# Turning the first four x tiles on TensorE, in a fused cross-attention and feed-forward kernel

## The chip, the cores and the metric

The kernel runs on one core of one Trainium2 chip. The metric is the device time of one execution in microseconds (us). A few times are given in nanoseconds (ns). Engines are named as in the profile: PE is TensorE's matmul, PEld its weight load, DVE is VectorE, ACT is ScalarE, POOL is GpSimd, SP is SyncE, and SPq is SyncE's queue, which issues all DMAs here.

## The reference

Two batches of x (1024 x 2048, f32) and of a context ctx (2048 x 2048, f32). Each passes through two blocks with a residual:

```python
def fake_quant(x, s, z):
    return (clip(round(x / s + z), 0, 255) - z) * s

x = x + fake_quant(layernorm(x), s1, z1) @ fake_quant(ctx, s2, z2)
xf = layernorm(x)
# router: softmax over 8 experts, the two largest, scaled to sum 1 -> w (zero elsewhere)
h = einsum('td,erd->ter', xf, lora_A)
lora = einsum('ter,eor,te->to', h, lora_B, w) * 2.0
x = x + xf @ W_base.T + b_base + lora
```

The change touches only the first line: the layernorm of x, its quantisation and the way it gets to TensorE in the first product.

## The kernel before

A tile is 128 rows of x, so a batch has eight, i = 0 to 7. The first product (GEMM1) contracts over 2048 rows of ctx, 16 steps of 128, named k. It writes four column blocks of 512, named c0 to c3. One unit (i, c) is 16 matmuls of 128x128 by 128x512 into one PSUM bank. All matmuls take f16; the quantised values are small integers.

**From x to the stationary operand (ln1).** Each tile is loaded in two halves of 1024 columns (h = 0, 1); tile 0 of batch 0 in four pieces. VectorE takes batch statistics (L387) and a first guess of the reciprocal root (L393 to L401). Newton steps refine it (L412 to L423), and three small operations (L616 to L618) make scale and offset. [...] Then ScalarE writes q as uint8, which rounds and clips, and ScalarE or VectorE subtracts the zero point and writes qn as f16. The matmul needs the tile with k on the partitions, so a DMA transpose (L356, on SyncE's queue) writes aT (in the profile `at`). Tile 0 of batch 0 has one for each half, every other tile one for the whole:

```python
            if b == 0 and i == 0:
                transpose(... HD)      # one for each half h
        if b or i:
            transpose(aT.ap, qn.ap, [qn], [aT], D)
```

**From ctx to the moving operand (load_b).** Each column block is loaded in eight parts of 512 KB (`bs`, L352). For each part, one operation writes u as uint8 and one writes b as f16. Both go through `affine` (L366 on ScalarE, L375 and L377 on VectorE), which the planner may put on either engine.

**Warm-up.** When the first half of qn of tile 0 is there, TensorE runs WARM = 30 matmuls on it, whose result is not used.

**GEMM1 and after.** gemm1 issues a unit in groups of two or four k (L670), and VectorE adds the result to x (L691). Batch 0 goes through tiles 0 to 3 for all four columns first, then 4 to 7. After a tile's four units comes its second layernorm (ln2, y_prep): f32 combinations, split into a high and a low f16 part (`nat`) and turned by a DMA transpose (`y`). The second product (GEMM2, L1119) is a Strassen-like scheme over those, with the weight prepared in the same way (w_step, L931), after a short one for the router (hmm, `ph`, L819 and L823). w_norm reads the whole weight once for a scale (`wn`).

**Order.** The kernel's body only adds tasks to a Plan: for each task an engine or a choice of engines, an assumed duration, the buffers it reads and writes, and a priority. Priorities are due times, worked backwards from the due time t of the matmuls. Plan.order then plays the program through greedily. At each moment every free engine takes the ready task with the smallest priority that fits into the buffers. The instructions are issued in the order that comes out, and each engine runs its own in order, so that an instruction which waits holds all those behind it. For a DMA transpose the plan lets SyncE be busy until all earlier DMAs have landed. The warm-up task has priority 0.0. Buffers come from slots: 48 of 4 KB per partition (`u`), and eight PSUM banks (`ps`).

Of the kernel before, what the change touches and what calls it, by code (L numbers as in the profile page):

```python
# [12 lines left out]
F16 = mybir.dt.float16  # L13
# [8 lines left out]
P = 128  # L22
# [7 lines left out]
HK = KT // 2  # L30
# [4 lines left out]
HD = D // 2  # L35
# [9 lines left out]
LANES = 8  # L45
DEPTH = 2.5
NEAR = 45.0
WARM = 30
WFAR = 90.0
HFIRST = (0, 2, 4)  # L50
HLATE = (6, 1, 3, 5, 7)
EV1 = 5.0
SP_D = 10.0
HC = 4.0
PUT = 10.0
# [36 lines left out]
class Plan:  # L92
# [3 lines left out]
    def add(self, eng, dur, fn, r=(), w=(), prio=None, cap=None, dma=None, far=None, turn=False):  # L96
        t = Task()
        t.durs = eng if isinstance(eng, dict) else {eng: dur}
        t.eng, t.dur = None, min(t.durs.values())
        t.fn, t.prio, t.cap, t.dma = fn, prio, cap, dma  # L100
        t.preds, t.succs, t.bufs = set(), [], []
        t.seq, t.ready, t.start, t.done = len(self.tasks), 0.0, None, None
        t.pe = prio if eng == "PE" else None
        t.far, t.turn = far, turn

        def spans(accs):
            for a in accs:
                buf, parts = a if isinstance(a, tuple) else (a, None)
                if buf not in t.bufs:
                    t.bufs.append(buf)  # L110
                    buf.users += 1
                for i in range(buf.parts) if parts is None else parts:
                    yield buf, i

        for buf, i in spans(r):
            last, readers = buf.state[i]
            if last is not None:
                t.preds.add(last)
            readers.append(t)
        for buf, i in spans(w):  # L120
            last, readers = buf.state[i]
            if last is not None:
                t.preds.add(last)
            t.preds.update(readers)
            buf.state[i] = (t, [])
        t.preds.discard(t)
        for p in t.preds:
            p.succs.append(t)
        self.tasks.append(t)
        return t  # L130
# [14 lines left out]
    def order(self):  # L145
        self.rank()
        free = dict(SLOTS)
        busy = dict.fromkeys(("SP", "ACT", "DVE", "POOL", "PE"), 0.0)
        ready = {e: [] for e in busy}
        events = [0.0]  # L150
        lanes = []
        dma_free = 0.0
        land = 0.0
        lag = 0.0
        for t in self.tasks:
# [5 lines left out]
        first = set()  # L161
# [36 lines left out]
        while todo:  # L198
# [8 lines left out]
            for eng in busy:  # L207
                while busy[eng] <= now:
                    pick = None
                    q = ready[eng]  # L210
                    for n, item in enumerate(q):
                        t = item[2]
                        if t.ready > now:
                            continue
                        h = t.far if t.far is not None else HORIZON
# [19 lines left out]
                    t = pick  # L235
# [9 lines left out]
                    if t.dma is not None:  # L245
                        if t.turn:
                            end = max(end, land)
                            dma_free = max(dma_free, end + t.dma)
# [33 lines left out]
def xattn_ffn_kernel(ctx, tc, x, cx, scal, wT, bias, arT, bT, out):  # L282
    nc = tc.nc
# [13 lines left out]
    def bank(name):  # L297
        return Buf(
            "ps", lambda: psum.tile([P, C], F32, tag="mm", bufs=SLOTS["ps"], name=name),
            name=name,  # L300
        )

    def fixed(t, parts=1):
# [26 lines left out]
        out=ident, in_=ident, pattern=[[-1, P]], compare_op=ALU.not_equal, fill=1.0, base=0,  # L330
        channel_multiplier=1,
    )
    iota = const.tile([P, E], F32)
    for e in range(E):
        nc.gpsimd.memset(iota[:, e : e + 1], float(e))
# [19 lines left out]
    def transpose(dst, src, r, w, cols, **kw):  # L355
        add("SP", 1.35 + 0.25 * cols / 1024, lambda: nc.sync.dma_start_transpose(dst(), src()),  # L356
            r=r, w=w, dma=0.5 * cols / 1024, turn=True, **kw)

    def affine(dst, src, n, r, w, scale=None, bias=None, only=None, **kw):
        ptrs = sum(v is not None and not isinstance(v, float) for v in (scale, bias))  # L360

        def fn(eng):
            get = lambda v: v() if callable(v) else v
            o, i, a, c = dst(), src(), get(scale), get(bias)
            if eng == "ACT":
                nc.scalar.activation(  # L366
                    o, i, AF.Copy if c is None else AF.Identity,
                    scale=1.0 if a is None else a, bias=0.0 if c is None else c,
                )
            elif a is None and c is None:  # L370
                nc.vector.tensor_copy(o, i)
            elif c is None:
                nc.vector.tensor_scalar(o, i, a, None, ALU.mult)
            elif a is None:
                nc.vector.tensor_scalar(o, i, c, None, ALU.add)  # L375
            else:
                nc.vector.tensor_scalar(o, i, a, c, ALU.mult, ALU.add)  # L377

        durs = {"ACT": n * 0.00083 + 0.19 + 0.09 * ptrs, "DVE": n * 0.00053 + 0.145 + 0.06 * ptrs}
        if only:  # L380
            return add(only, durs[only], lambda: fn(only), r=r, w=w, **kw)
        return add(durs, 0, fn, r=r, w=w, **kw)
# [217 lines left out]
    def ln1(S, b, i):  # L600
        n = f"{b}_{i}"
        xt = S["x", i]
        s = buf("sm", [P, 52], F32, f"sm1_{n}")
        for h in range(2):
            add("DVE", 1.3, lambda h=h: stats(xt[h], s, 0, h), r=[xt[h]], w=[s])
        add("DVE", 0.8, lambda: rstd_seed(s, 1), w=[s])

        fast = b == 0 and i == 0

        def newton():  # L610
            e = nc.vector if fast else nc.gpsimd
            rstd_newton(e, s, 1)
            a = s.ap()
            r = a[:, 4:5]
            m = a[:, 48:49]
            e.tensor_tensor(a[:, 10:11], r, r1, ALU.mult)  # L616
            e.tensor_tensor(a[:, 11:12], m, a[:, 10:11], ALU.mult)
            e.tensor_tensor(a[:, 12:13], z1, a[:, 11:12], ALU.subtract)  # L618

        add("DVE" if fast else "POOL", 2.2 if fast else 4.0, newton, w=[s])  # L620
        aT = buf("u", [P, KT, P], F16, f"at_{n}", 2)
        qn = buf("u", [P, D], F16, f"qn_{n}", 2)
        for h in range(2):
            q8 = buf("q8", [P, HD], U8, f"q8_{n}_{h}")
            affine(q8.ap, xt[h].ap, HD, [xt[h], s], [q8],
                   scale=lambda: s.ap()[:, 10:11], bias=lambda: s.ap()[:, 12:13],
                   only="ACT")
            affine(lambda h=h: qn.ap()[:, h * HD : (h + 1) * HD], q8.ap, HD, [q8], [(qn, [h])],
                   bias=nz1)
            if b == 0 and i == 0:  # L630
                transpose(
                    lambda h=h: aT.ap()[:, h * HK : (h + 1) * HK, :],
                    lambda h=h: qn.ap()[:, h * HD : (h + 1) * HD],
                    [(qn, [h])], [(aT, [h])], HD)
        if b or i:
            transpose(aT.ap, qn.ap, [qn], [aT], D)
        S["at", i] = aT
        if fast:
            warm = bank("warm")

            def warm_up():
                for _ in range(WARM):
                    nc.tensor.matmul(
                        warm.ap(), qn.ap()[:, :P], qn.ap()[:, :C], start=True, stop=True
                    )

            add("PE", MM * (WARM + 8), warm_up, r=[(qn, [0])], w=[warm], prio=0.0)

    def load_b(S, b, c):
        for j in range(4):  # L650
# [627 lines left out]
```

## Time and profile before

| what | us |
|---|---|
| median of 3 runs (957.34 to 962.02) | 958.4 |
| the profiled execution | 959.11 |
| its span in the profile | 957.3 |
| PE busy | 909.2 |
| DVE busy | 712.4 |
| ACT busy | 418.9 |
| POOL busy | 85.1 |

The mean granted clock of TensorE in the profiled execution is 0.994 of full speed. The queue of DMAs carries 242.33 MB and takes 83.7% of the 16 DMA engines' span; HBM moves 213 GB/s over the span. Before the first matmul of the warm-up there are 17.03 us, and the first of GEMM1 starts at 25.30.

In the profile's rows a time in brackets is how long the engine sat idle before that row, with what released it. A wait for several things is put down to the one that came last. Idle time of an engine that is not the bottleneck costs nothing by itself. Windows of a few microseconds count the DMA share of 16 engines, so a value near 1 is a full stretch.

### The profile page before, as it was taken

Reading aid. Unit: us, or ns where it says so; the run is one execution under the profiler, and the core shown is the slowest. Engines: PE = TensorE matmul, PEld = TensorE weight load, DVE = VectorE, ACT = ScalarE, POOL = GpSimd, SP = SyncE. Lnnn points to the kernel's source line nnn. Section 1 sums busy time; section 2 is a strip of 40 time slices with the busy share of each in tenths; the row PEclk is TensorE's granted clock in tenths of the full one; section 3 lists DMA queues with packets and bytes.
Section 4 is the critical chain, followed back from the end, with each engine's and each line's share of the span. In section 5 each row is a group of like instructions: output and inputs, shape, how many; then the busy total and the mean of one; then the engine's idle time right before and its main releaser. Section 6 shows DMA issues by size and latency. Waiting matters only on the chain.

```text
span 957.3 us, 12424 instructions
## 1 busy us (share of the span) xinstructions
PE 909.2 (95%) x4484; PEld 431.6 (45%) x4484; DVE 712.4 (74%) x1224; ACT 418.9 (44%) x473; POOL 85.1 (9%) x352
## 2 busy tenths in 40 slices
PE   2799998999989999999999999998999999999998
PEld 1244445465434444444444444644644444444443
DVE  7579758998878885999464765899938996599331
ACT  4598658823436242333566664671611331224000
POOL 2305212000000000003320122000000000000000
PEclk9999999999999999999999999999999999999999
DMA  9899999699999999966899858899795779893011
GB/s 315 225 391 353 271 304 262 158 217 296 199 311 332 355 339 352 353 206 227 229 252 374 339 155 235 212 218 223 248 226 194 232 243 343 296 382 126 34 70 63
DMA packets 231534, 243.12 MB, mean 254 GB/s; under 512 B 160816, under 2 KB 162864, under 8 KB 231472
## 3 DMA queue, kind: packets, MB, share of 16 engines
q1 hardware_dynamic: 231472, 242.33, 83.7%
q8 instruction: 35, 0.57, 0.2%
q14 instruction: 27, 0.22, 0.1%
HBM read 172.03 MB, written 31.46 MB: 213 GB/s over the span
## 4 chain that ended last, share of the span: by engine, by line
PE 49%; DVE 21%; DMA 18%; issue 5%; POOL 4%; SPq 1%; ACT 1%; DVEq 0%; ACTq 0%; POOLq 0%
PE X L1119 19%; PE Y L1119 13%; PE g L670 12%; DMA wb<-in_wT_dram 5%; DVE w L931 4%; DVE xr L1147 3%; DMA bs<-in_cx_dram 3%; DMA wt<-in_wT_dram 3%; DMA wn<-in_wT_dram 3%; PE ph L819 2%; DMA wc<-in_wT_dram 2%; DVE wb L999 2%; DVE xr L1038 2%; PE X L1135 1%; PE ph L823 1%
## 5 line engine op out<-in xcount | busy, mean ns | idle before, releaser
L670 PE MATMUL g<-b,at 128*128 128x512 f16 x1024 | 225.3, 381 | 9.9 <-DMA at<-qn 7.4
L1119 PEld LDWEIGHTS <-y_s 128*128 128x128 f16 x1536 | 150.2, 98 | 185.9 <-issue 5.6
L1119 PE MATMUL X<-w,y_s 128*128 128x512 f16 x768 | 206.9, 379 | 4.4 <-DVE w L931 2.9
L1119 PE MATMUL Y<-w,y_s 128*128 128x512 f16 x768 | 206.9, 379 | 0.1
L1119 PE MATMUL X<-w,y_a 128*128 128x512 f16 x768 | 189.9, 379 | 3.2 <-DVE w L931 1.6
L1119 PEld LDWEIGHTS <-y_a 128*128 128x128 f16 x1152 | 112.3, 98 | 138.8 <-issue 7.0
L670 PEld LDWEIGHTS <-at 128*128 128x128 f16 x1024 | 100.2, 98 | 132.2 <-DMA at<-qn 9.4
L366 ACT ACTIVATE w<-wb,gW 128x1024 f16<-128x1024 f32 (+1 forms) x64 | 66.0, 1039 | 156.4 <-DVE wb L992 45.8
L1119 PE MATMUL Y<-w,y_a 128*128 128x512 f16 x384 | 103.8, 381 | 1.6 <-DVE xr L1147 1.6
L931 DVE SCALAR_TENSOR_TENSOR w<-wb,gW,w 128x1024 f16<-128x1024 f32 (+1 forms) x64 | 73.0, 1148 | 9.2 <-ACT w L366 9.1
L1147 DVE SCALAR_TENSOR_TENSOR xr<-X,uW,xr 128x512 f32<-128x512 f32 x64 | 46.5, 745 | 30.2 <-PE X L1135 28.7
L366 ACT ACTIVATE u<-bs,sc,rec 128x1024 uint8<-128x1024 f32 x45 | 55.5, 1238 | 25.8 <-DMA bs<-in_cx_dram 23.2
L691 DVE SCALAR_TENSOR_TENSOR x<-g,s,x 128x512 f32<-128x512 f32 x64 | 47.2, 746 | 12.3 <-PE g L670 12.2
L1147 DVE SCALAR_TENSOR_TENSOR xr<-Y,uW,xr 128x512 f32<-128x512 f32 x42 | 31.1, 744 | 31.8 <-PE Y L1135 31.8
L375 DVE TENSOR_SCALAR b<-u,nz 128x1024 f16<-128x1024 uint8 x40 | 29.9, 752 | 29.2 <-ACT u L366 29.1
L366 ACT ACTIVATE w<-wc,gW 128x1024 f16<-128x1024 f32 x23 | 26.2, 1143 | 54.9 <-DVE wc L955 45.4
L387 DVE BATCH_NORM_STATS2 sm<-x 128x6 f32<-128x512 f32 x64 | 40.7, 682 | 12.1 <-DMA x<-in_x_dram 6.2
L366 ACT ACTIVATE q<-x,sm 128x1024 uint8<-128x1024 f32 x32 | 38.5, 1231 | 24.0 <-POOL sm L618 15.0
L412 POOL TENSOR_SCALAR sm<-sm 128x1 f32<-128x1 f32 (+1 forms) x21 | 4.5, 216 | 482.9 <-DVE sm L399 421.2
L709 ACT ACTIVATE sq<-x,sm 128x1024 uint8<-128x1024 f32 x32 | 36.4, 1138 | 19.7 <-DVE sm L702 10.9
L819 PE MATMUL ph<-ar,y_a 128*128 128x272 f16 x192 | 38.2, 292 | 7.0 <-DMA y_a<-nat_a 4.1
L366 ACT ACTIVATE nat_s<-yt_a 128x1024 f16<-128x1024 f32 x32 | 33.0, 1049 | 19.6 <-DVE yt_a L778 11.2
(168 smaller groups left out, 970.6 us busy)
## 6 DMA issues: line engine op xcount, KB each, us to landing
wt<-in_wT_dram SPq DMA_DIRECT2D x80, 512.0 KB, 6.7
bs<-in_cx_dram SPq DMA_DIRECT2D x64, 512.0 KB, 10.5
wn<-in_wT_dram SPq DMA_DIRECT2D x32, 512.0 KB, 8.7
wb<-in_wT_dram SPq DMA_DIRECT2D x32, 512.0 KB, 6.9
x<-in_x_dram SPq DMA_DIRECT2D x30, 512.0 KB, 8.7
spill<-x SPq DMA_DIRECT2D x28, 512.0 KB, 3.8
xr<-spill SPq DMA_DIRECT2D x28, 512.0 KB, 8.3
wc<-in_wT_dram SPq DMA_DIRECT2D x24, 512.0 KB, 7.9
```

Source lines behind the costliest of these rows:

```text
L366: nc.scalar.activation(o, i, AF.Copy if c is None else AF.Identity, scale=1.0 if a is None else a, bias=0.0 if c is None else c,)
L375: nc.vector.tensor_scalar(o, i, c, None, ALU.add)
L387: nc.vector.bn_stats(st[:, 2 * h + c], b.ap()[:, c * C : (c + 1) * C])
L670: nc.tensor.matmul(ps.ap(), aT.ap()[:, k, :], S["b", c, k // 4].ap()[:, k % 4, :], start=k == 0, stop=k == KT - 1,)
L691: nc.vector.scalar_tensor_tensor(xs, ps.ap(), s12, xs, ALU.mult, ALU.add, accum_out=s.ap()[:, o : o + 1])
L709: nc.scalar.activation(sq.ap(), xb.ap(), AF.Square, bias=a[:, 22 + j : 23 + j], accum_out=a[:, 24 + 2 * j + h : 25 + 2 * j + h],)
L819: nc.tensor.matmul(ph.ap()[:, : 2 * AR], y[half].ap()[:, 0, k, :], ar[:, kr, :], start=kk == 0, stop=False,)
L931: lambda: nc.vector.scalar_tensor_tensor(w.ap()[:, 1, lo:up], src(), g, w.ap()[:, 0, lo:up], ALU.mult, ALU.subtract),
L999: lambda: nc.vector.tensor_tensor(bot.ap(), bot.ap(), top.ap(), ALU.subtract),
L1038: lambda xb=xb: nc.vector.tensor_tensor(xb.ap(), xb.ap(), bb.ap(), ALU.add),
L1119: nc.tensor.matmul(ps.ap(), y.ap()[:, a, k, :], w.ap()[:, q, j * C : (j + 1) * C], start=k == 0 and fresh and i == 0, stop=k == HK - 1 and ...
L1147: nc.vector.scalar_tensor_tensor(xs, ps.ap(), uW[:, cp : cp + 1], xs, ALU.mult, ALU.add)
```

## The change

For tiles 0 to 3 of batch 0 (TURNS = 4) the DMA transposes fall away. In their place comes `turn`, once for each half: eight TensorE transposes of 128x128, with an f16 identity made once by GpSimd, into one PSUM bank read as f16, and one `affine` that copies the bank to aT, on ScalarE or VectorE. For the same four tiles the Newton chain runs on VectorE; before, that held for tile 0 alone. The warm-up has 20 matmuls instead of 30. The planner starts all engines at 0.9 us and its DMA clock at 1.2 us. Tiles 4 to 7 of batch 0, all of batch 1, and the transposes of y stay with the DMA.

```diff
-WARM = 30
+WARM = 20
...
+TURNS = 4
+TMM = 0.12
...
-        busy = dict.fromkeys(("SP", "ACT", "DVE", "POOL", "PE"), 0.0)
+        busy = dict.fromkeys(("SP", "ACT", "DVE", "POOL", "PE"), 0.9)
...
-        events = [0.0]
+        events = [0.0, 0.9]
...
-        dma_free = 0.0
+        dma_free = 1.2
...
+    ident16 = const.tile([P, P], F16)
+    nc.gpsimd.tensor_copy(ident16, ident)
...
-        fast = b == 0 and i == 0
+        first = b == 0 and i == 0
+        pe_turn = fast = b == 0 and i < TURNS
...
-            if b == 0 and i == 0:
-                transpose(
-                    lambda h=h: aT.ap()[:, h * HK : (h + 1) * HK, :],
-                    lambda h=h: qn.ap()[:, h * HD : (h + 1) * HD],
-                    [(qn, [h])], [(aT, [h])], HD)
-        if b or i:
+            if pe_turn:
+                turn(aT, qn, h, n)
+        if not pe_turn:
             transpose(aT.ap, qn.ap, [qn], [aT], D)
         S["at", i] = aT
-        if fast:
+        if first:
             warm = bank("warm")
...
+    def turn(aT, qn, h, n):
+        ps = bank(f"turn_{n}_{h}")
+
+        def mm():
+            for j in range(HK):
+                k = h * HK + j
+                nc.tensor.transpose(
+                    ps.ap().bitcast(F16)[:, j * P : (j + 1) * P],
+                    qn.ap()[:, k * P : (k + 1) * P], ident16,
+                )
+
+        add("PE", HK * TMM, mm, r=[(qn, [h])], w=[ps])
+        affine(
+            lambda: aT.ap()[:, h * HK : (h + 1) * HK, :].rearrange("p k t -> p (k t)"),
+            lambda: ps.ap().bitcast(F16), HD, [ps], [(aT, [h])])
```

## The prediction

> **What bounds the kernel now.** I read the page's busy shares first, then the waits of TensorE, then the timelines of TensorE, of SyncE's queue and of ScalarE over the first 60 us, and last the windows around them. Busy shares:
>
> ```profile
> span 957.3 us, 12424 instructions
> PE 909.2 (95%) x4484; PEld 431.6 (45%) x4484; DVE 712.4 (74%) x1224; ACT 418.9 (44%) x473; POOL 85.1 (9%) x352
> ```
>
> TensorE is idle for 957.3 - 909.2 = 48.1 us in all, so an edit that leaves its matmuls alone can win only from these and from matmuls at a low clock. Its waits (engine and line, what it waited for, total us, times, longest):
>
> ```profile
> PE warm L643 <- ACT qn L366: 17.0, 1, 17.0
> PE g L670 <- DMA at<-qn: 7.4, 4, 3.9
> PE ph L819 <- DMA y_a<-nat_a: 4.1, 2, 3.4
> PE g L670 <- DVE b L375: 1.9, 2, 1.3
> ```
>
> The 17.0 us are the first tile's way to qn, which the change leaves as it is. The next row is the landing of the DMA transposes. TensorE's timeline shows where it lies (start, length, what, and in brackets the idle time before it):
>
> ```profile
> 17.03 8.44 PE L643 MATMUL warm<-qn 128*128 128x512 f16 x30 [17.03 <-ACT qn L366]
> 25.30 1.89 PE L670 MATMUL g<-b,at 128*128 128x512 f16 x8
> 31.11 6.07 PE L670 MATMUL g<-b,at 128*128 128x512 f16 x20 [3.92 <-DMA at<-qn]
> 37.71 2.75 PE L670 MATMUL g<-b,at 128*128 128x512 f16 x12 [0.53 <-DVE b L375]
> 42.89 7.08 PE L670 MATMUL g<-b,at 128*128 128x512 f16 x32 [2.43 <-DMA at<-qn]
> 51.30 29.12 PE L670 MATMUL g<-b,at 128*128 128x512 f16 x134 [1.33 <-DVE b L375]
> ```
>
> By 51.30 only 8+20+12+32 = 72 matmuls are done. In the last row one takes 29.12/134 = 0.217 us, so 72 are worth 15.6 us, yet they took 26.0. The 20 at 31.11 took 6.07 instead of 4.34: the clock had dropped in the gap before. Why the transposes are late stands in SyncE's queue and in ScalarE:
>
> ```profile
> 18.40 3.33 SPq L352 DMA_DIRECT2D bs<-in_cx_dram  x4
> 25.02 15.47 SPq L356 DMA_TRANSPOSE at<-qn  x4
> 40.55 14.68 SPq L352 DMA_DIRECT2D bs<-in_cx_dram  x15
> ...
> 28.05 1.24 ACT L366 ACTIVATE q<-x,sm 128x1024 uint8<-128x1024 f32 x1 [1.90 <-POOL sm L618]
> 34.24 1.24 ACT L366 ACTIVATE q<-x,sm 128x1024 uint8<-128x1024 f32 x1 [2.68 <-POOL sm L618]
> ```
>
> Four transposes stand in the queue one behind another, each waiting for its qn, and from 21.7 to 40.55 no context load goes out behind them. The qn wait for GpSimd's Newton steps: its three chains run from 16.15 to 20.60, to 28.02 and to 34.21, 4.5, 7.5 and 6.2 us. The windows show what it leaves empty (length, busy time of PE, PEld, DVE, ACT, POOL with counts, clock, DMA share, GB/s):
>
> ```profile
> 30.00:40.00 10.00, 8.36 (x31) 3.43 (x32) 6.48 (x12) 6.10 (x6) 3.48 (x10) 0.83 0.47 96
> 60.00:70.00 10.00, 10.00 (x48) 4.52 (x47) 8.73 (x20) 9.83 (x12) 0.00 (x0) 1.00 1.04 392
> ```
>
> The DMA engines are half empty just before a stretch in which they are full (share 1.04) and VectorE and ScalarE nearly so.
>
> **Part by part.** *Removed: five DMA transposes and GpSimd's three Newton chains.* Gone are 3.92 + 2.43 us of waits for at. The waits for b at 37.71 and 51.30 (0.53 + 1.33) come from loads held back behind the transposes: gone with the block, if ScalarE and VectorE convert in time. Gone is the cold clock: 6.07 - 4.34 = 1.7 us. Sum 8.2 + 1.7 = 9.9 us.
>
> *Added on VectorE: three Newton chains.* The first tile's chain, already there, runs from 12.45 to 14.52: 2.07 us, so 6.2 us for three. On GpSimd the same cost 18.2 us, and it was on the path. Queued behind each in VectorE's order are the next tile's statistics (0.64 us each) and the conversions of b.
>
> *Added on TensorE: 64 transposes of 128 columns, in 8 groups of 8.* No row shows one. From below: a 128x136 matmul at L823 is followed by the next after 0.057 us (155.02 to 155.08), 56 x 0.057 = 3.2 us; I count 7 groups, since the first runs ahead of the first matmul. From above: nothing overlaps, and each pays its weight load (0.098 us) and the full length of a 128x136 matmul (0.223 us), 56 x 0.32 = 17.9 us. I take 0.0875 us, half the 0.175 us in which a pair of L819 and L823 with two weight loads repeats, since a transpose needs one load for few columns: 4.9 us. A gain is excluded: it is pure extra work on the engine that sets the end.
>
> One rule speaks against the change. The Trainium skill, "TensorE: Matmul & The Clock Gate", Part 4: PE-mode transpose, gives about 275 ns for a 128x128 transpose inside a kernel and says that transposes don't count as activity for the clock gate. By that the term would be 56 x 0.275 = 15.4 us, an estimate, and the whole change a loss of 3.5 us. This trace shows no transpose; I hold to its rows, because eight in a row to one bank can be pipelined as the pairs at L819 are.
>
> *Added on ScalarE or VectorE: eight evacuations of 128x1024 f16 from PSUM.* Bounds: 0.75 us (L375, as many elements) and 1.23 us (L366 from f32); at 1.0 that is 8 us. With Newton it makes 14.2 us of new work. From 25.3 to 51.3 ScalarE was busy for 13.34 of 26.0 us and VectorE for 12.46, so 26.2 us lie free: it fits, but the c1 conversions (8 parts at 1.23 + 0.75, 16 us) move into the same stretch. 14.2 + 16 exceeds 26.2 by 4 us of two engines, 2 us of time. I charge these 2.0 us as new waits for b or at; bounds 0 and 5.
>
> *Warm-up 20 instead of 30.* The ten dropped matmuls ran at 0.217: 2.2 us, so it ends at 25.47 - 2.2 = 23.3. It has priority 0.0 and stands before the first turn in TensorE's order. Turn 0.7, evacuation 0.75 to 1.15 and some hops: first real matmul at 25.0 to 25.4. Before, it was 25.30. I count nothing: the ten matmuls only hid the transpose's landing.
>
> *Moved: the context loads, up to 19 us earlier.* DMA is full from 40 to 170, and a tile's transpose kept it about 2.4 us (share 0.47 of 10 us for two from 30 to 40). So the work behind runs ahead of need. The small waits later in GEMM1 (0.65 at 81.07, 0.49 at 89.06, 0.15 at 100.63, 0.90 at 104.29; sum 2.2) should mostly go: 1.5 us. At the seam to GEMM2 TensorE waits 4.1 us for y_a; ScalarE, which prepares it, waited 8.2 us for wn loads from 100 to 165. With those earlier I take 2.5 us of the 4.1, bounds 0 and 4.1. What is late next is the chain of the last tile's layernorm, which doesn't depend on loads.
>
> *The planner's clock* starts at 0.9 us for all engines. A uniform shift changes no order by itself. But new durations reorder the greedy plan, and from 164 us on TensorE still idles for 48.1 - 17.0 - 14.5 = 16.6 us, spread over many waits. That can move by about 3 us either way; I count 0. The identity's f16 copy on GpSimd comes at about 2 us, 15 us before use: free.
>
> Sum against the profiled execution's 959.1 us (its span is 957.3): -9.9 + 4.9 + 2.0 - 1.5 - 2.5 = -7.0, so 952.1. The median of the runs is 0.7 lower than that execution, 958.4: 951.4, rounded to **951.5**.
>
> **The rivals.** *The converters take over.* Without the DMA in the way ScalarE and VectorE hold the first two columns, and TensorE waits for b instead of at. For it: 9 tenths busy from 60 to 90. Against: 26 us free before. With 5 us of new waits and nothing won at the seam: -9.9 + 4.9 + 5.0 - 1.5 = -1.5, about 957.
>
> *The transposes don't pipeline.* Place: TensorE's own queue between 23 and 45 us, where seven groups stand between matmuls. At 0.32 us each: -9.9 + 17.9 + 2.0 - 1.5 = +8.5, about 967. It decides from (9.9 - 2.0 + 1.5)/56 = 0.17 us per transpose on. For it: a single 128-column matmul has a length of 0.22 us. Against: the rows at L819 and L823 follow one another at a quarter of that.
>
> *Everything comes back.* Waits for at, the four small ones and the seam go entirely, and transposes cost 0.057: -9.9 - 2.2 - 4.1 + 3.2 = -13, about 945.
>
> *It doesn't do what it says*, if the turns stand in order behind a late qn and hold ready matmuls. TensorE would then wait as long as now; about 958, the same side as the first rival.
>
> **How the numbers follow.** Forecast 0.47 (its own range 948 to 955), everything back 0.18, converters or late qn 0.25, no pipelining 0.10. What a measurement of this kernel can tell from no change is about 0.5%, 4.8 us: faster means below 953.6, slower above 963.2. The forecast gives 0.43 to faster and 0.04 to same; everything back 0.18 to faster; the first rival 0.01 to faster, 0.23 to same and 0.01 to slower; no pipelining 0.10 to slower. Faster 0.62, same 0.27, slower 0.11. The range 944 to 960 leaves out most of the no-pipelining case and the ends of others.
>
> **What would show it.** Right: no wait for at before 55 us, first real matmul near 25, context loads without a gap from 20 to 40, transposes at under 0.12 us from one to the next, 128 matmuls done by about 60 instead of 63.5. Wrong: waits for b of over 5 us in all before 60, or a seam wait larger than 4.1 us, or groups of eight transposes longer than 1.4 us.

## The result, and the profile after

| | before | after |
|---|---|---|
| median of 20 runs each, same chips, us | 959.83 (956.35 to 964.44) | 959.14 (956.49 to 961.82) |
| ratio of after to before, 95% interval | | 0.9989 (0.9977 to 1.0002) |
| span of the profiled execution, us | 957.3 | 957.2 |

No difference that this kernel's measurement can tell, where 951.5 and faster were forecast. The page after, busy shares:

```profile
span 957.2 us, 12516 instructions
PE 912.3 (95%) x4538; PEld 434.5 (45%) x4538; DVE 716.7 (75%) x1255; ACT 423.7 (44%) x480; POOL 71.4 (7%) x305
```

TensorE has 54 matmuls more (64 transposes, 10 warm-up matmuls less), GpSimd is busy 13.7 us less. TensorE's waits (columns as before):

```profile
PE warm L645 <- DVE qn L379: 16.9, 1, 16.9
...
PE Y L1137 <- DVE x L1165: 2.8, 1, 2.8
PE ph L837 <- DMA y_a<-nat_a: 2.7, 2, 1.9
PE X L1137 <- DVE x L1165: 2.5, 1, 2.5
PE g L688 <- DVE b L379: 2.1, 1, 2.1
...
PE turn L657 <- ACT qn L370: 1.2, 1, 1.2
PE g L688 <- ACT at L370: 0.8, 2, 0.6
```

The 7.4 us for `DMA at<-qn` are gone, and what took their place before 60 us is small (2.1 for b, 1.2 for qn, 0.8 for at, now copied by ScalarE). But far behind the change, Y at L1137 waits 2.8 us for VectorE's x at 220 us, which has no counterpart in before, and X waits 2.5 us for it at 769 us, where before waited 1.5:

```profile
PE X L1119 <- DVE x L1147: 1.5, 1, 1.5
```

TensorE's timeline of after at the start:

```profile
23.09 0.61 PE L657 MATMUL turn<-ident,qn 128*128 128x128 f16 x8
24.89 0.62 PE L657 MATMUL turn<-ident,qn 128*128 128x128 f16 x8 [1.20 <-ACT qn L370]
25.80 1.04 PE L688 MATMUL g<-b,at 128*128 128x512 f16 x4 [0.28 <-ACT at L370]
...
29.99 0.59 PE L688 MATMUL g<-b,at 128*128 128x512 f16 x2 [2.06 <-DVE b L379]
...
43.13 40.43 PE L688 MATMUL g<-b,at 128*128 128x512 f16 x186
```

Eight transposes take 0.61 us. One has a length of 0.219 us in the trace, so from one to the next it is (0.61 - 0.219)/7 = 0.056 us. From 43.13 on the matmuls run in one block of 186. SyncE's queue sends the context loads without a hole, 23 from 7.72 to 39.05, and the window from 30 to 40, which had a DMA share of 0.47, is full:

```profile
7.72 31.33 SPq L356 DMA_DIRECT2D bs<-in_cx_dram  x23
```

```profile
30.00:40.00 10.00, 9.44 (x60) 5.12 (x60) 9.48 (x16) 10.00 (x11) 0.00 (x0) 0.83 1.05 387
60.00:70.00 10.00, 10.00 (x48) 4.51 (x46) 10.00 (x21) 9.97 (x12) 3.55 (x11) 1.00 1.04 394
```

**Where the time went.** The order of the instructions behind 156 us is the same on all engines in both kernels, and the matmuls are the same in number, so the n-th can be compared with the n-th. The table gives its start minus that in the first profile of before, us (warm-up, transposes and added dummies not counted; negative is earlier); the columns are the time that this matmul has in before. Kernels below the second row are those of the experiments.

| kernel | 25 | 62 | 113 | 185 | 242 | 353 | 627 | 767 | 953 |
|---|---|---|---|---|---|---|---|---|---|
| after | +0.5 | -2.4 | -5.8 | **-8.1** | -5.2 | -3.7 | -3.7 | -3.0 | **-0.4** |
| after, a second profile (e5) | +0.5 | -2.4 | -5.7 | -7.8 | -3.2 | -3.5 | -3.7 | -3.9 | -1.5 |
| before, a second profile (e9) | 0.0 | -0.3 | -0.2 | -1.9 | -2.1 | +0.4 | +0.2 | +0.7 | +0.1 |
| loads on ScalarE's queue (e1) | +0.1 | -2.8 | -6.1 | -6.9 | -7.2 | -3.3 | -2.7 | -3.4 | -3.3 |
| start 8 us later (e3) | +8.6 | +5.7 | +2.4 | +1.2 | +1.7 | +4.2 | +4.7 | +6.0 | +8.5 |
| Newton alone (e4) | +0.6 | -2.9 | -4.8 | -6.8 | -6.7 | -4.8 | -5.0 | -4.4 | -5.2 |
| turn alone (e10) | -0.1 | +0.9 | -2.4 | -7.4 | -3.6 | -2.1 | -1.9 | -1.2 | +2.2 |
| after, 74 dummies (e13) | +0.4 | -2.5 | -5.8 | -8.7 | -7.5 | -5.6 | -6.1 | -5.5 | -5.5 |
| Newton alone, 54 dummies (e14) | +0.8 | -3.1 | -4.2 | -4.0 | -4.2 | -1.2 | -1.6 | -2.7 | -1.9 |
| before, 54 dummies (e16) | -0.4 | -1.2 | -1.0 | -0.4 | -0.6 | +1.6 | +1.3 | +0.9 | +1.6 |

The gain is there at 185 us, 8.1 us, more than the 7.0 forecast. Then it is given back: 2.8 us by 242, 1.6 by 353, 0.6 by 767 and 2.7 just behind it. The third row says how far to trust one row: two profiles of the same kernel stand up to 2.1 us apart at these columns, though these two agree at the end (the two of after end 1.1 us apart).

**The loss at 220.** SyncE's queue ahead of it, before and after:

```profile
210.18 0.53 SPq L352 DMA_DIRECT2D wt<-in_wT_dram  x1
210.76 3.32 SPq L356 DMA_TRANSPOSE y_s<-nat_s  x1
...
220.96 0.53 SPq L352 DMA_DIRECT2D wt<-in_wT_dram  x1
```

```profile
202.79 0.96 SPq L356 DMA_DIRECT2D wt<-in_wT_dram  x1
203.80 5.24 SPq L360 DMA_TRANSPOSE y_s<-nat_s  x1
...
215.94 0.53 SPq L356 DMA_DIRECT2D wt<-in_wT_dram  x1
```

The first wt load goes out 7.4 us earlier than before, but the transposition behind it holds the queue for 5.24 us instead of 3.32, and the next wt load goes out only 5.0 us earlier. VectorE waits for that one, and TensorE for VectorE:

```profile
220.65 0.69 DVE L964 TENSOR_TENSOR wb<-wt 128x512 f32<-128x512 f32 x1 [1.72 <-DMA wt<-in_wT_dram]
...
222.40 0.74 DVE L1165 SCALAR_TENSOR_TENSOR x<-Y,uW,x 128x512 f32<-128x512 f32 x1
```

```profile
223.19 0.81 PE L1137 MATMUL Y<-w,y_s 128*128 128x512 f16 x3 [2.75 <-DVE x L1165]
```

So the first 2.8 us went into a transfer that was never on TensorE's path in the forecast. Before had the same wait of VectorE, with TensorE far enough behind for it not to matter:

```profile
225.88 0.69 DVE L946 TENSOR_TENSOR wb<-wt 128x512 f32<-128x512 f32 x1 [1.67 <-DMA wt<-in_wT_dram]
```

The size of TensorE's wait is about what its lead (8.1 us) exceeds the lead of that wt load by (5.0). Why the transposition ahead of it takes longer is the question of the last experiments.

### The profile page after: what moved, and what is told of

It reads as the page before. It is cut to its first block, busy times and chain, and to the rows that moved or that the text cites. A ratio compares the mean times of both kernels' runs of the same rounds, so it can differ in the third digit from the quotient of the medians.

```text
span 957.2 us, 12516 instructions
## 1 busy us (share of the span) xinstructions
PE 912.3 (95%) x4538; PEld 434.5 (45%) x4538; DVE 716.7 (75%) x1255; ACT 423.7 (44%) x480; POOL 71.4 (7%) x305
## 4 chain that ended last, share of the span: by engine, by line
PE 62%; DVE 18%; DMA 11%; issue 3%; SPq 3%; ACT 3%; POOL 1%; DVEq 0%; ACTq 0%
PE X L1137 23%; PE g L688 18%; PE Y L1137 16%; DMA wb<-in_wT_dram 5%; DVE w L949 3%; SPq L360 2%; DVE xr L1165 2%; DMA wc<-in_wT_dram 2%; DMA wn<-in_wT_dram 2%; PE X L1153 2%; DVE nat_s L789 2%; DVE xr L1056 1%; PE ph L837 1%; DVE wb L979 1%; DVE sm L391 1%
## 5 line engine op out<-in xcount | busy, mean ns | idle before, releaser
L1137 PEld LDWEIGHTS <-y_s 128*128 128x128 f16 x1536 | 150.5, 98 | 188.8 <-issue 9.9
L1137 PE MATMUL X<-w,y_s 128*128 128x512 f16 x768 | 207.7, 380 | 2.9 <-ACT w L370 1.4
L1137 PE MATMUL Y<-w,y_s 128*128 128x512 f16 x768 | 207.5, 380 | 2.9 <-DVE x L1165 2.8
L1137 PE MATMUL X<-w,y_a 128*128 128x512 f16 x768 | 192.0, 382 | 4.8 <-DVE x L1165 2.5
L1137 PEld LDWEIGHTS <-y_a 128*128 128x128 f16 x1152 | 112.7, 98 | 142.0 <-issue 11.5
L1137 PE MATMUL Y<-w,y_a 128*128 128x512 f16 x384 | 103.8, 381 | 1.6 <-DVE xr L1165 1.6
L370 ACT ACTIVATE u<-bs,sc,rec 128x1024 uint8<-128x1024 f32 x47 | 57.5, 1234 | 17.8 <-DMA bs<-in_cx_dram 13.4
L561 ACT ACTIVATE wn<-wn 128x1024 f32<-128x1024 f32 x22 | 23.2, 1053 | 45.6 <-DMA wn<-in_wT_dram 45.6
```

Of the source, the lines that this page charges most:

```text
L370: nc.scalar.activation(o, i, AF.Copy if c is None else AF.Identity, scale=1.0 if a is None else a, bias=0.0 if c is None else c,)
L561: nc.scalar.activation(d.ap(), s.ap(), AF.Square, accum_out=o)
L1137: nc.tensor.matmul(ps.ap(), y.ap()[:, a, k, :], w.ap()[:, q, j * C : (j + 1) * C], start=k == 0 and fresh and i == 0, stop=k == HK - 1 and ...
```

## The experiments

Times are medians, in brackets the ratio to runs of before on the same chip and its 95% interval. The texts on record name their theories by letters of their own; the verdicts below are in words.

**e1 and e2, the weight loads of the second group on ScalarE's queue.** In the kernel after (e1) and, as a control, in the kernel before (e2), the loads wt and wb of group 1 are issued by ScalarE, so that no transposition stands ahead of them:

```diff
-    def load(dst, dst_ap, src, nbytes, w, r=(), **kw):
-        add("SP", 0.42, lambda: nc.sync.dma_start(dst_ap(), src() if callable(src) else src),
+    def load(dst, dst_ap, src, nbytes, w, r=(), queue=None, **kw):
+        q = queue or nc.sync
+        add("SP", 0.42, lambda: q.dma_start(dst_ap(), src() if callable(src) else src),
...
+    Q1 = nc.scalar
...
-                top = load_wrow(k, cp, f"wt_{n}", far=WFAR)
+                top = load_wrow(k, cp, f"wt_{n}", far=WFAR, queue=Q1)
...
-                     C * 4, [(s, [0])])
+                     C * 4, [(s, [0])], queue=Q1)
```

> The changed kernel, with the weight loads of the second group of the second product (first column half, both batches) issued from ScalarE's queue instead of SyncE's; nothing else, same order. The changed kernel starts its second product 8.1 us earlier than the kernel before, and loses 2.8 us of that at one wait at 220 us, where VectorE waits for a weight load (wt) that stands in SyncE's queue behind two transposes of y. Theory A (the lead is lost at single places, each held by a chain that came forward less than TensorE): the wait of 2.8 us at 220 falls under 0.5, the lead after it stays at 7 to 8 us instead of 5.2, some of it is lost at the next place (320 us, the sum of the weight's squares), and the whole is 1 to 3 us below the changed kernel, about 956 to 958. Theory B (what follows is bound by the total work of the DMA engines and VectorE, so that any lead is lost): the lead is back at 5 us by 260, and the whole stays within 0.5 us of the changed kernel.

> The control for the run with weight loads on ScalarE's queue: the same edit on the kernel before. TensorE has no wait at that place there. Theory A: nothing to win at 220; total within 1 us of the kernel before, 958 to 960. Theory B: the same. A gain of over 2 us would mean that moving the loads is worth something by itself, and that the comparison has to be made against this kernel.

Measured: e1 957.13 (0.9974, 0.9953 to 0.9996), e2 959.42 (0.9982, 0.9962 to 1.0003). In e1 there is no wait at 220, and the lead stands at 242 with 7.2 us; in the kernel before the same edit changes nothing that is clear of noise. So the transfers on SyncE's queue make the wait at 220. By 353 the lead is nevertheless down to 3.3, where after has 3.7: what is saved at one join can be lost at the next.

**e3, TensorE later.** The kernel after with 37 more warm-up matmuls (`range(WARM + 37)`), nothing else.

> The changed kernel with 57 warm-up matmuls instead of 20, in an unchanged order: TensorE starts GEMM1 37 x 0.217 = 8.0 us later. Theory A: most of the 8 us is taken from a lead that would be lost anyway; the end moves by 0 to 3 us, to 959 to 962. Theory B: the same, 0 to 1 us. Rival C (waits after 184 us are fixed lengths of TensorE's own, as a sum of separate stalls would have it): the whole is 8 us slower, about 967.

Measured: 967.84 (1.0070, 1.0040 to 1.0100). The start is 8.1 us later than in after, the end 8.48 + 0.35 = 8.8 us. So TensorE's lead is not simply cut off by an engine that is no faster: at the end all of the delay is paid, as the rival in the expectation has it, and a lead ought to be kept in the same way. A later start also shifts where TensorE's code fetches fall (see e13), so this run does not separate the two.

**e4, Newton alone.** The kernel before, with the Newton steps of tiles 1 to 3 on VectorE; the DMA transposes and WARM = 30 stay.

```diff
-        fast = b == 0 and i == 0
+        fast = b == 0 and i < 4
+        first = b == 0 and i == 0
...
-        if fast:
+        if first:
             warm = bank("warm")
```

> The kernel before with one part of the change alone: the Newton steps of tiles 0 to 3 of batch 0 on VectorE, transposes still by DMA, 30 warm-up matmuls. It tells how much of the 8.1 us lead comes from Newton and how much from the turn. Expected: qn of tiles 2 and 3 come 4 to 8 us earlier, the block in SyncE's queue shrinks from 15.5 to about 10 us, and the lead at the start of the second product is 3 to 5 us. Theory A: less than 5.2 us of lead passes the place at 220 without loss; the whole is 0 to 2 us below the kernel before. Theory B: within 0.5 us of it. Rival C: 3 to 5 us below it.

Measured: 955.28 (0.9938, 0.9914 to 0.9961), clearly faster than before. Its waits in GEMM1 and its timeline at the start:

```profile
PE g L671 <- ACT b L366: 4.6, 3, 2.7
...
PE g L671 <- DMA at<-qn: 0.3, 1, 0.3
```

```profile
25.87 0.59 PE L671 MATMUL g<-b,at 128*128 128x512 f16 x2
28.16 0.59 PE L671 MATMUL g<-b,at 128*128 128x512 f16 x2 [1.69 <-ACT b L366]
31.46 28.73 PE L671 MATMUL g<-b,at 128*128 128x512 f16 x122 [2.71 <-ACT b L366]
```

With every DMA transpose in place TensorE waits 0.3 us for at instead of 7.4; its waits for b rise from 2.5 us to 4.6. The transposes were late because their qn were, behind GpSimd's chains; they were not slow. These few lines alone give 6.8 us of lead at 185, where the whole change has 8.1, and 5.2 of them reach the end. The turn adds up to 1.3 us of lead to that and costs VectorE and ScalarE 4 x 0.684 + 4 x 1.00 = 6.7 us of evacuations. VectorE's own lead at 150 us is 4.4 us in after and 4.8 in e4, no difference beside the spread of the profiles with Newton alone (3.7 to 4.9 in e4, e7 and e8).

**e5 to e9, what the difference is not.** e5 is the kernel after once more, e9 the kernel before once more (a single run). e6 adds five DMAs of 2 KB to the kernel after and e7 three to Newton alone, to turn SyncE's eight completion semaphores by as many places, since after issues five DMAs less than before. e8 is Newton alone with WARM = 20 and the planner's clock of the change.

> The changed kernel once more, unaltered, beside the next three runs. Newton alone ended 5 us below the changed kernel though its lead at the start of the second product is 1.3 us smaller, and a TensorE that starts 8.1 us later ended 8.8 us later: so a lead is not lost because other chains stand still. In the changed kernel 7.7 us go between 184 us and the end, with the same order of instructions there as before. Theory D (something of the changed kernel's own makes its waits after 184 us longer in every execution): the lead at 184 is again 8.1 within 0.5, the end again within 1 us of the kernel before, and the losses lie again at 220, at 320 to 340 and at 768 us. Theory E (single waits there differ from execution to execution, and what was read from one profile is partly chance): the losses lie at other places and the end differs by over 2 us from the first profile, while the median stays at that of the kernel before less 0 to 2 us.

> The changed kernel with five DMAs of 2 KB added on SyncE's queue, beside the first five turns, so that it issues as many DMAs as before. The DMAs of SyncE use eight completion semaphores in turn; with five DMAs fewer, every later DMA has another one than in the kernel before. Theory F (this shift makes the later waits longer): 3 to 5 us below the changed kernel, and a lead at the end of 4 to 5 us. Theories D and E: within 1.5 us of the changed kernel.

> The mirror of the last one: Newton on VectorE alone (transposes by DMA, 30 warm-up matmuls), with three DMAs of 2 KB added early, so that every later DMA has the completion semaphore that it has in the changed kernel. Theory F: 3 to 5 us above Newton alone. Theories D and E: within 1.5 us of it.

> Newton on VectorE alone, transposes by DMA, with the change's two other small parts added: 20 warm-up matmuls and the planner's start at 0.9 us. If these two cost the changed kernel its win, this one is 3 to 5 us above Newton alone; if it is the turn, this one stays within 1.5 us of Newton alone, and the turn is what is left.

> The kernel before once more, for a second profile. The losses after 184 us are counted against one execution of it. If that one was lucky somewhere, this one is later than it there by 1 to 3 us, with the same order of instructions: between 277 and 330 us first of all, where every kernel with an earlier start lost 2 to 3.5 us against it. If it is within 0.5 us of the first everywhere, those losses belong to the kernels.

Measured: e5 960.58 (0.9992, 0.9970 to 1.0014), e6 959.45 (0.9975, 0.9951 to 1.0000), e7 957.48 (0.9956, 0.9930 to 0.9982), e8 956.71 (0.9954, 0.9930 to 0.9977), e9 959.18. The transposition behind the wt load takes 5.29 us in e5 and 4.93 in e6, against 3.43 in e7 and 3.56 in e8, and only e5 and e6 wait at 220. So neither chance nor the semaphores, nor the warm-up or the planner's clock, lengthen that transposition; something that comes with the turn does. Newton alone stays faster than before in both forms.

**e10, the turn alone.** The kernel after with `fast = first`, so that the Newton steps of tiles 1 to 3 go back to GpSimd.

> The other part alone: tiles 0 to 3 turned by TensorE, with 20 warm-up matmuls and the planner's start at 0.9 us, but the Newton steps of tiles 1 to 3 on GpSimd as before. Theory G (what reaches the end is the lead of VectorE's chain with the weight loads it waits for; the turn brings forward TensorE alone and gives VectorE and ScalarE more to do): TensorE's lead at 184 is 2 to 5 us, VectorE's lead after 241 us is 1 to 2 us smaller than that, and the whole is within 3 us of the kernel before, 957 to 961. Rival H (the turn by itself is worth what the loads in SyncE's queue gain): lead of 4 to 6 us at 340, whole at 954 to 956.

Measured: 960.57 (0.9986, 0.9968 to 1.0004). Its longest wait in GEMM1 is for at, as in before, through another engine:

```profile
PE g L689 <- ACT at L370: 5.1, 2, 4.4
```

It stands at 185 with 7.4 us of lead, has the wait at 220 too (2.2 us; its transposition: 5.38 us), and ends 2.2 us behind. So the lead at 185 alone does not tell the two halves apart, 6.8 us with Newton and 7.4 with the turn; what is left of it at the end does. At 220 the arithmetic is that of after: TensorE's 7.4 us meet a wt load that goes out only 5.4 us earlier than in before (215.55 for 220.96).

**e11 and e12, Newton alone with other queues.** e11: the loads of e1 on ScalarE's queue. e12: in its place the wn loads of the second half (`queue=nc.scalar if cp else None`).

> A candidate that may beat both: Newton on VectorE alone (transposes by DMA, 30 warm-up matmuls), and the weight loads of the second group on ScalarE's queue. Newton alone has no wait at 220, so theory G expects little there, 0 to 2 us below Newton alone, at 953 to 956; if weight loads behind transposes of y also hold back VectorE's chain, 2 to 4 below.

> Newton on VectorE alone, and the 16 loads for the second column half's sum of squares (wn, 270 to 320 us) on ScalarE's queue. In every kernel with an earlier start TensorE waits 1.9 to 2.7 us for that sum near 320. If the wait is the loads' turn in SyncE's queue, it falls under 1 us and the whole is 1 to 2 us below Newton alone; if it is the DMA engines' own pace there (share 1.0), nothing changes, within 1 us.

Measured: e11 954.84 (0.9934, 0.9909 to 0.9960), the lowest time of the study, but not told apart from e4. e12 960.93 (1.0002, 0.9976 to 1.0027): its lead went from 4.6 us to none between matmul 1205 and 1220 of the real work (264 to 272 us), where TensorE waits for transpositions of y (2.0 and 0.8 us). Which of the moved loads did it wasn't followed up.

**e13 to e16, the code fetches.** The DMA view of the kernel after for 204 to 210 us shows what the page hides (40 slices of 0.15 us; then the queues with packets, MB and share):

```profile
DMA  9999754559995979996999994000000000059999
...
q1 hardware_dynamic: 1818, 0.94, 115.3%
q8 instruction: 1, 0.02, 1.0%
```

From 207.75 to 209.25 next to no packet starts on the 16 engines, and the one packet of q8 in this window is 16 KB of code that starts at 207.61. The same row of before, for the same window, has nine empty slices from 206.55 on, behind a fetch at 206.21; there it falls on another transposition. The trace of every kernel here holds 35 or 36 such packets, on average one for every 128 matmuls with their weight loads: TensorE's code. 64 transposes more and 10 warm-up matmuls less shift all of them:

| kernel | two fetches, at matmul of the real work | at us | transposition behind wt, us |
|---|---|---|---|
| before | 828, 954 | 206.2, 218.8 | 3.32 |
| Newton alone (e4) | 830, 956 | 199.7, 212.2 | 3.44 |
| after | 766, 923 | 186.3, 207.6 | 5.24 |
| turn alone (e10) | 766, 917 | 186.9, 207.8 | 5.38 |

The Trainium skill, page "Runtime: NRT & Kernel Launch", section "Instruction fetch mechanics", says that an engine's code streams in by blocks of 16 KB (256 instructions) over a DMA queue of its own, and calls the cost mostly hidden. The rows of q8 agree with the block, and TensorE has no wait from 204 to 212 us in after; it is the other transfers that stand still.

To move the fetches alone, small matmuls on zeros go ahead of the warm-up, where TensorE has nothing to do for 16 us: 74 in after (e13, fetches back to where before has them), 37 (e15), and 54 in Newton alone (e14) and in before (e16), as many as the whole change adds.

```diff
+    pad16 = const.tile([P, P], F16)
+    nc.gpsimd.memset(pad16, 0.0)
...
             def warm_up():
+                for _ in range(74):
+                    nc.tensor.matmul(
+                        warm.ap()[:, :8], pad16, pad16[:, :8], start=True, stop=True
+                    )
```

> The kernel after, with 74 small matmuls (8 columns each, on a tile of zeros) put ahead of the warm-up, while TensorE has nothing to do. They change nothing but the number of instructions in TensorE's stream, and so the places at which its code is fetched. In the traces one 16 KB code fetch (queue 8) comes for about every 128 matmuls with their weight loads: in the kernels with the turn one falls at about matmul 766 and the next at about 918 (207 us), with those weight loads and transpositions in flight; in the kernels without it at about 830 and 955 (200 and 212 us). Theory F (the added TensorE instructions moved a code fetch onto the transfers that the seam at 220 needs): with 74 more the fetches are back at about 826 and 955; the transposition behind the wt load takes 3.3 to 3.6 us instead of 5.2, no wait over 1 us at 220, the lead of 8 us stands at 242 with 7 or more, and the time is 955 to 957, 2 to 4 us under the kernel after. Theory L (the converters' later chain makes that wait, or chance): 2.5 to 3.3 us of wait at 220 as before, and 959 to 960.

> The kernel with the Newton steps alone, with 54 small matmuls ahead of the warm-up: as many instructions more as the turn adds to TensorE's stream. Theory F: code fetches at about matmul 770 and 920, so that one falls on the transfers at 204 to 209 us, a wait of 2 to 3.3 us at 220 that this kernel did not have, and 957 to 959 instead of 955.3. Theory L: no wait at 220, and 955 to 956 as without them.

> The kernel after with 37 small matmuls, half of the shift back: code fetches at about matmul 728 and 880, so at about 181 and 203 us, ahead of the wt load. Theory F: the wait at 220 is gone or under 1.5 us, and the time 956 to 958. Theory L: the wait of about 3 us stands, 959 to 960.

> The kernel before with 54 small matmuls: the code fetches stand where the turn puts them, with none of the rest of the change. Theory F: fetches at about matmul 770 and 920; the seam's transfers come 7 us later here, at 210 to 218 us, and TensorE does not lead so far, so the fetch at 920 (214 us) falls on them as well: a wait of 1 to 3 us at about 226, and 960 to 963. Theory L: the time of the kernel before, 959 to 961, and no wait there.

Measured: e13 956.07 (0.9968, 0.9946 to 0.9990), e14 957.19 (0.9976, 0.9950 to 1.0002), e15 960.89 (1.0012, 0.9988 to 1.0036), e16 963.10 (1.0038, 1.0011 to 1.0065). In e13 the fetches come at matmul 828 and 963 (197.6 and 211.3 us), and the same stretch of DMA, queue and TensorE reads:

```profile
DMA  1679499399999999999999999916976889999999
...
q1 hardware_dynamic: 3076, 1.42, 99.2%
```

```profile
202.14 0.94 SPq L358 DMA_DIRECT2D wt<-in_wT_dram  x1
203.14 3.49 SPq L362 DMA_TRANSPOSE y_s<-nat_s  x1
...
213.44 0.53 SPq L358 DMA_DIRECT2D wt<-in_wT_dram  x1
```

```profile
220.89 0.81 PE L1143 MATMUL Y<-w,y_s 128*128 128x512 f16 x3 [1.23 <-DVE x L1171]
```

No hole, no row of q8, 3.49 us for the transposition, and TensorE goes on 2.3 us earlier than in after (220.89 for 223.19). 7.5 us of the lead stand at 242 and 5.5 at the end of this profile, which is the fastest of e13's twelve runs (953.84). So the place of the fetch makes that transposition long and most of the wait at 220. Not all of it: no wait over 1 us was expected, and 1.23 us stay, as TensorE's lead of 8.7 us meets a wt load that leads by 7.5 (213.44 for 220.96). In e4 the two leads are 6.8 and 6.7, and there is no wait.

The transposition just ahead of the first wt load says the same of the fetches: it takes 1.95 us in after and 1.98 in e13, but 3.37 in e15 and 3.67 in e4, where a fetch falls on it (at 202.3 and 199.7 us).

The rest of the expectations held in part. e16 shows that the shift costs time with none of the rest of the change (its interval lies above 1). e14's median is 1.9 us above e4's, but its interval overlaps those of e4, e7 and e8. Neither has the wait at 220 that was expected of them; they pay in smaller portions elsewhere, e14 already before 185 and again by 353, e16 between 284 and 299 us. And e15, expected at 956 to 958, is the slowest form of after: its fetch only moved to the transposition ahead of wt, the next wt load goes out hardly earlier than in after (215.53 for 215.94), and 1.85 us of wait at 220 are left.

The wait behind 767 is shorter in e13 too, 1.48 us for 2.50, and the clock differs behind it. The windows from 766 to 778 (columns as before; the clock stands ahead of the last two) of after and of e13:

```profile
766.00:772.00 6.00, 3.50 (x17) 1.41 (x15) 6.00 (x9) 0.72 (x1) 0.00 (x0) 0.97 0.71 231
772.00:778.00 6.00, 6.00 (x22) 2.40 (x21) 5.76 (x9) 2.06 (x3) 0.00 (x0) 0.75 0.68 216
```

```profile
766.00:772.00 6.00, 4.52 (x22) 1.97 (x21) 6.00 (x8) 1.14 (x2) 0.00 (x0) 1.00 0.69 216
772.00:778.00 6.00, 6.00 (x29) 2.73 (x28) 5.10 (x8) 3.52 (x4) 0.00 (x0) 1.00 0.79 267
```

After the wait of 2.50 us the clock was 0.75 and 22 matmuls ran in 6 us; after the shorter one 1.00 and 29. That makes 7 x 0.217 = 1.5 us. But the length of the wait does not decide it alone. In e15 the same matmul waits longer still, and the clock stays at 1.00:

```profile
775.01 7.28 PE L1143 MATMUL X<-w,y_a 128*128 128x512 f16 x33 [2.90 <-DVE x L1171]
```

```profile
775.00:781.00 6.00, 5.99 (x28) 2.74 (x28) 5.76 (x8) 1.88 (x3) 0.00 (x0) 1.00 0.82 267
```

In e8, on the other hand, 2.05 us were enough for 0.72 (770 to 776 us). What else decides was not tested.

**e17 and e18, the two that were left.** e17 is after with the edits of e1 and e13 together; e18 is the turn alone (e10) with the 74 dummies.

> The kernel after with both edits that gave time back: the weight loads of the second group on ScalarE's queue, and the 74 small matmuls that set TensorE's code fetches back. If the two losses are separate and add (957.1 with the loads moved, 956.1 with the fetches moved, 959.1 to 960.6 with neither), 953 to 955, as good as the Newton steps alone with the same loads moved (954.8) or a little better. If they are the same loss told twice, 956 to 957.

> The turn on TensorE with the Newton steps of tiles 1 to 3 on GpSimd, and the 74 small matmuls, so that the code fetches stand where the kernel before has them. If the place of the fetches costs the same 0.2 to 0.4% in every kernel (0.38% in the kernel before, 0.2 to 0.4% with the Newton steps alone, 0.1 to 0.2% in the kernel after), the turn alone, 0.9986 with its own fetches, comes to 0.995 to 0.997, that is 955 to 957. If the place of the fetches matters only in some kernels by chance, it stays at 0.998 to 0.999, 958 to 960.

Measured: e17 956.38 (0.9943, 0.9911 to 0.9976), e18 958.63 (0.9979, 0.9958 to 1.0000). e17 is not told apart from e13, 956.07: there is no sign of two losses that add. In e18 the fetches stand right (matmul 821 and 951), the transposition takes 3.77 us, and it is still not at 955 to 957: TensorE has a lead of 7.0 us at 185, VectorE one of 3.4 at 150, and by 353 nothing is left. The four combinations, with the fetches in both places:

| | fetches near 828, 955 | fetches near 766, 918 |
|---|---|---|
| neither half | 1 (before) | 1.0038 (e16) |
| Newton alone | 0.9938 (e4), 0.9956 (e7), 0.9954 (e8) | 0.9976 (e14) |
| turn alone | 0.9979 (e18) | 0.9986 (e10) |
| both | 0.9968 (e13) | 0.9989 (after), 0.9992 (e5), 0.9975 (e6) |

The medians of each row are slower on the right, by 0.07 to 0.38%. Most single intervals are wide enough to overlap (about 0.2% to either side); only the first row is clear by itself. In the left column Newton alone has the lowest ratios, though e13's interval overlaps theirs.

## Why the prediction was wrong

**Right.** The waits for at before 55 us fall from 7.4 us to 0.8, these two for ScalarE's copy (none was forecast); the first real matmul starts at 25.80 (25.0 to 25.4 was forecast); the context loads run without a gap; the transposes stand 0.056 us apart, at the lower bound of 0.057 and not at the chosen 0.0875, so that the rival of transposes that don't pipeline falls, as does the price of 275 ns that the prediction weighed. Waits for b come to 2.1 us, not over 5: the converters did not take over.

**The sum up to the seam, by the table of leads.** To 62 us it was -9.9 + 4.9 + 2.0 = -3.0, measured -2.4. That it comes so near is in part luck. The 1.7 us for the clock did not come: from 30 to 40 us it is 0.83 as before, with waits of 2.06 and 0.56 us around 30 now. Against that, six groups of transposes, not seven, stand between matmuls, and from each one's start to the next matmul's they take 3.1 us in all, not 4.9. GEMM1's rest was -1.5, measured -5.8 + 2.4 = -3.4. The seam was -2.5, measured -8.1 + 5.8 = -2.3; the waits for y_a alone fell by 1.4 (4.1 to 2.7). Together -7.0 forecast, -8.1 measured.

**The step that failed** is the one for the time from 164 us on: 16.6 us of idle time that "can move by about 3 us either way; I count 0". From the same matmul on (164.05 us in before, 155.94 in after) TensorE is idle for 21.9 us instead of 16.4, and busy for 779.3 us instead of 776.8 with the same 3841 matmuls (the clock is lower in places, as behind 767): 8.0 us, nearly all of the lead, where the sum had nothing. Two thoughts led to it. "So the work behind runs ahead of need" was read from the start of the kernel, where the DMA queue had been held back; at 220 us VectorE waited 1.7 us for a weight load in before and in after alike, and a TensorE that comes 8 us earlier meets that load. And the transposes were charged to TensorE at their own time, 4.9 us, and to nothing else: as instructions they shift the later fetches of TensorE's code (those at matmul 828 and 954 come at 766 and 923), and one fetch fell on the transfers of the seam. Set back, it gives 2.3 us at 220. In the whole time the ratios differ by 0.7 to 2.3 us (0.9968 against 0.9975 to 0.9992), with intervals that overlap. So of the 7.7 us that the table loses between 185 and 953 the 2.8 at 220 are traced to their causes, and the rest is not.

**The credit was in the wrong half.** The prediction read rightly that the qn wait for GpSimd's Newton steps, and took the removed waits as the gain of transposes and chains together. e4 shows that moving the chains takes the waits for at from 7.4 us to 0.3, and keeps 5.2 us of lead to the end. The turn alone (e10) takes them to 5.1 only and keeps nothing. What the turn adds to the chains is at most 1.3 us of lead for TensorE, against 6.7 us of evacuations for two engines that were full (9.48 and 10.00 of 10 us) and another 54 matmuls of code. With both halves and the fetches set back, e13 at 0.9968 is not better than the Newton steps alone at 0.9938 to 0.9956.

**What stays open.** The losses around 280, 320 and 767 us vary from profile to profile by 1 to 3 us, also between two runs of one kernel, and no run took a single one of them apart. The loss between 242 and 353 may not be the change's at all: the second profile of before (e9) loses 2.5 us against the first there. Why one 16 KB packet, 0.97 us long itself, goes with 1.5 us of standstill is not shown; in after the packets thin out some 0.4 us before it starts. Nor is it shown why the fetches cost 0.38% in before and only 0.07% with the turn alone, or why e15 is slower than after behind 242.

## What to carry to other kernels

Before pricing a change with several parts, ask which part alone would remove the wait: here a late producer, not a slow transpose, and moving its few small operations (e4, e7 and e8, ratios of 0.9938 to 0.9956) is clear of before each time and has lower ratios than all three of the changed kernel (0.9975 to 0.9992). A lead is only a gain if the engines and queues that feed the later joins get it too; look up each later wait that was hidden by the old lateness. And when an engine's instruction count changes, compare where its code fetches fall among the transfers, or shift them with idle dummies, before explaining a small difference by the edit itself.

## What the runs showed of the hardware

- A fetch of TensorE's code is a 16 KB packet among the data transfers, on average one for 128 matmuls with weight loads. Around the one at 207.6 us all 16 DMA engines stood nearly still for 1.5 us, and packets that had started just before took up to 2.8 us. A transposition of y that met a fetch took 3.4 to 3.7 us instead of 2.0 (e15 and e4 against after and e13), or 5.2 instead of 3.5 (after against e13). 54 idle matmuls at the start, where TensorE only waits, made the kernel before 0.38% slower.
- TensorE's transposes of 128x128 f16, eight in a row into one bank, follow each other at 0.056 us (0.219 us each in length). The Trainium skill, page "TensorE: Matmul & The Clock Gate", Part 4, gives about 275 ns for one in a kernel; for a row of them the measured spacing is the price.
- A Newton chain with the three operations behind it is ten small instructions on VectorE and took 2.07 us there; on GpSimd it is sixteen and took 4.5 to 7.5 us. Moving three such chains made the kernel 0.4 to 0.6% faster (e4, e7, e8).
- Behind a wait of 2.50 us TensorE's clock was 0.75 over the following 6 us, and behind one of 2.05 (e8) 0.72; behind one of 2.90 (e15) it stayed at 1.00. The length of a wait does not tell by itself whether the clock falls.
